# Ordering the work of an attention loop: from one fixed round per step to an order written by a planner with costs and due times

## The chip, the core and the metric

The kernel runs on one core of a Trainium2 chip. The core has five instruction streams that matter here: TensorE (PE in the profile, with PEld for its weight loads), VectorE (DVE), ScalarE (ACT), GpSimd (POOL) and SyncE (SP), which issues the transfers. Each stream executes its own instructions strictly in the order in which the program wrote them, and waits on semaphores for the other streams. The metric is the device time of one execution in microseconds (us), the median of several runs. Lower is better.

## What is computed

One block: a layer norm of `x` (4096 x 512) and of a context (3202 x 512), cross attention with 8 heads of 64, a residual, a second layer norm, and then a small recurrence over the 4096 rows. All of it is in 32-bit floats.

```python
x = _layernorm(builder_state, g1, beta1)
base_n = _layernorm(base_state, g1, beta1)
scores = jnp.einsum('bhqd,bhkd->bhqk', q, k) * (1.0 / np.sqrt(HD))
attn = jax.nn.softmax(scores, axis=-1)
out = jnp.einsum('bhqk,bhkd->bhqd', attn, v)
x = residual + out.reshape(q_in.shape) @ W_o.T + b_o
U = (_layernorm(x, g2, beta2) @ W_in.T + b_in) @ Bmat
s = silu(s @ A.T) + u_t            # 4096 steps in a row, 64 states
x = residual + states @ Cmat + mod
```

The change leaves every one of these operations, with its operands and shapes, as it is.

## The kernel before, in words

**Three parts.** First the keys and values of all 3202 context rows are made and stored in device memory (up to about 260 us of the span). Then comes the attention loop, to about 2510 us. Last, the recurrence runs, with what is left of the last rows (to 2587 us).

**The attention loop.** The 4096 queries are cut into 8 blocks Q of 512; a block has 4 pairs of heads (hp) and 2 halves of 256 queries. One (Q, hp, half) is a *unit*: 64 units. The keys are cut into 13 chunks of 2 x 123 or 2 x 124. One chunk of one unit is a *step*: 832 steps. A step has these pieces, each on one engine:

- `scores` (L465, PE): four matmuls of q and k into a PSUM tile `s` of two banks; there are two such tiles. In the trace a 32-bit matmul is two records, so a piece is x8.
- then a copy of `s` into an SBUF tile `p` (L475, ACT). Up to 20 tiles `p` are alive (NDC + LAG + 4).
- `running` (L486, DVE): the running maximum `top` of the unit, from `s` and the last `top`. It waits for the copy. When it is done, the PSUM tile is free.
- `subtract` (L520, DVE): `p` less the maximum of the unit, `mb`, which lies in PSUM.
- `weights` (L530, ACT): the exponential in place, and, in the same function, `acc` (L539, POOL): the sum of the exponentials over the chunks, an add of 123 x 1024 numbers. The first chunk needs none, so a unit has 12.
- `product` (L548, PE): four matmuls of `p` and v into the PSUM tile `po`. Then `p` is free.

The subtraction needs the maximum over all 13 chunks, so a unit's second half of work (subtract, weights, product) runs 16 to 18 steps (NDC + LAG) behind its scores. Between them lies, once per unit, `maximum`: eight transposes `tt` (L497), two reductions (L504), four transposes `mb` (L512). After a unit's last product comes `finish`: `po` copied (L595, ACT), the two halves of `acc` added (`both`, L598, POOL), transposes `pd` (L604), a reciprocal (L609, L610), a spread (`wide`, L612, ACT), transposes `rb` (L617), a multiplication (L623, DVE).

**Background work.** Per block Q there are two streams. `queries(Q + 1)` loads and normalizes four tiles of x, transposes them (L141) and makes the q of the next block: four times sixteen records `pq` (L180). `project(Q)` takes four tiles of 128 rows through: load, POOL add of `rowb` (L635), matmuls `pa` with the output weights (L638), DVE add (L647), layer norm, POOL add of `modb` (L650), store on SP's queue (L656), transposes `tp_y`, copy (L660), matmuls `pu` (L667), DVE (L671).

**What sets the order.** One Python loop over the steps g, the *round*, writes for each g the same list: the loads of k (4 steps ahead) and v, `running` of step g-1, `weights` of step g-17, `scores` of g, `subtract` of g-16, `product` of g-18, and then at most one portion of each background stream (`background`, which takes the next `yield` of a generator; a stream holds a PSUM tile `m` at most across one portion). So each engine gets its work in the round's fixed order, PE always scores, product, background, and so again; nothing looks at costs.

**Names the change touches.** `queries`, `normalize`, `scores`, `running`, `maximum`, `weights`, `product`, `finish`, `project`, the loop itself. The loop is L1020. The tail (`main_scan` L867, `last_rows` L906) is left, but for how its first pieces are written out.

Of the kernel before, what the change touches and what calls it, by code (L numbers as in the profile page):

```python
# [1 line left out]

# [6 lines left out]
F32 = mybir.dt.float32  # L9
# [21 lines left out]
L = 16  # L31
# [5 lines left out]

def keys(c):
    return CK if c < GC else CK - 1


def key0(c):
    return c * (CK - 1) + min(c, GC)


@with_exitstack
def xattn_ssm_kernel(
# [64 lines left out]
    def normalize(xt, n, name, later=False, pool=None):  # L112
# [5 lines left out]
        nc.vector.bn_aggr(mv[:n], st[:n])  # L118
        ve = pool.tile([P, 1], F32, tag="ve", name=f"ve_{name}")
# [6 lines left out]
        )  # L126

        def scaled():
            xh = pool.tile([P, H], F32, tag="xh", name=f"xh_{name}")
            nc.scalar.activation(  # L130
                xh[:n], xt[:n], AF.Identity, bias=nmr[:n], scale=rstd[:n]
            )
            return xh

        return scaled if later else scaled()
# [16 lines left out]
    def queries(Q, fetched=None):  # L152

        xns = []
        for half in range(2):
            xn = xnp.tile([P, NC, QU], F32, tag="xn", name=f"xn_{Q}_{half}")
            xns.append(xn)
            for t in range(NT // 2):
                r = Q * QB + half * QU + t * P
                if fetched:  # L160
                    xt = fetched[:, half * (NT // 2) + t, :]
                else:
                    xt = xp_.tile([P, H], F32, tag="x", name=f"x_{r}", bufs=3)
                    nc.sync.dma_start(xt, x[r : r + P, :])
                    yield False
                scaled = normalize(xt, P, f"x{r}", later=True)
                yield False
                yield False
                xh = scaled()
                yield False  # L170
                tp = transposes(ps_m, "m", xh, P, f"x{r}")
                yield True
                nc.scalar.copy(xn[:, :, t * P : (t + 1) * P], tp)
                yield False
                yield False
        for hp in range(NC):
            pq = ps_m.tile([P, 512], F32, tag="m", name=f"pq_{Q}_{hp}")
            for half in range(2):
                for i in range(NC):
                    nc.tensor.matmul(  # L180
                        pq[:, half * QU : (half + 1) * QU],
                        wq[:, i, hp * P : (hp + 1) * P],
                        xns[half][:, i, :],
                        start=(i == 0),
                        stop=(i == NC - 1),
                    )
            yield True
            t = qp.tile([P, QB], F32, tag="q", name=f"q_{Q}_{hp}")
            nc.scalar.activation(
                t, pq, AF.Identity, bias=bias[:, hp : hp + 1], scale=HD**-0.5  # L190
            )
            qt[Q, hp] = t
            yield False
# [50 lines left out]
    def side():  # L244
# [95 lines left out]
        yield from queries(0, x0)  # L340
# [117 lines left out]
    def scores(w, c):  # L458
# [3 lines left out]
        for b in range(2):  # L462
            for a in range(2):
                r = slice(a * HD, (a + 1) * HD)
                nc.tensor.matmul(  # L465
                    s[:n, a, b, :],
                    kts[(*w["at"][:2], c)][r, b * n : (b + 1) * n],
                    q[r],
                    start=True,
                    stop=True,  # L470
                )
        t = sp_.tile([CK, 2, 2, QU], F32, tag="s", name=f"p_{w['name']}_{c}")
        w["s"][c] = t
        w["ps"] = s
        nc.scalar.copy(t[:n], s[:n])  # L475

    def running(w, c):

        n, s = keys(2 * c), w["ps"]
        if c == 0:  # L480
            w["top"] = w["s"][0]
            return
        before = w["top"]
# [4 lines left out]
    def maximum(w):  # L488

        m = small.tile([P, 2, 2], F32, tag="m", name=f"m_{w['name']}")  # L490
        tps = []
        for t in range(2):
            tp = ps_m.tile([P, 2, 2, CK], F32, tag="m", name=f"tt_{w['name']}_{t}")
            tps.append(tp)
            for a in range(2):
                for b in range(2):
                    nc.tensor.transpose(  # L497
                        tp[:, a, b, :],
                        w["top"][:, a, b, t * P : (t + 1) * P],
                        ident[:CK, :CK],  # L500
                    )
        yield
        for t in range(2):
            nc.vector.tensor_reduce(  # L504
                m[:, t, :], tps[t].rearrange("p a b k -> p a (b k)"), AX.X, ALU.max
            )
        yield
        mb = ps_b.tile([P, 2, QU], F32, tag="b", name=f"mb_{w['name']}")
        w["mb"] = mb
        for t in range(2):  # L510
            for a in range(2):
                nc.tensor.transpose(  # L512
                    mb[:CK, a, t * P : (t + 1) * P],
                    m[:, t, a : a + 1].to_broadcast([P, CK]),
# [12 lines left out]
    def weights(w, c):  # L527
# [3 lines left out]
        if w["last"] and c in PE_SUMS:  # L531
            return
        before = w.get("acc")
        if before is None:
            w["acc"] = t
            return
# [4 lines left out]
    def product(w, c):  # L541

        n, t = keys(2 * c), w["s"].pop(c)
# [11 lines left out]
        if w["last"] and c in PE_SUMS:  # L555

            if c == PE_SUMS[0]:
                w["pd"] = ps_m.tile([P, 512], F32, tag="m", name=f"pd_{w['name']}")
            sums(w["pd"], t, n, c == PE_SUMS[0], False)
# [29 lines left out]
    def finish(w):  # L589

        Q, hp, half = w["at"]
        name = w["name"]
# [3 lines left out]
        acc = w["acc"]  # L596
        both = accp.tile([CK, 2, QU], F32, tag="both", name=f"both_{name}", bufs=1)
        nc.gpsimd.tensor_tensor(both, acc[:, :, 0, :], acc[:, :, 1, :], ALU.add)  # L598
        yield False
        yield False  # L600
        pd = ps_m.tile([P, 2, 2, CK], F32, tag="m", name=f"pd_{name}")
        for t in range(2):
            for a in range(2):
                nc.tensor.transpose(  # L604
                    pd[:, t, a, :], both[:, a, t * P : (t + 1) * P], ident[:CK, :CK]
                )
        yield True
        rd = small.tile([P, 2, 2], F32, tag="rd", name=f"rd_{name}")
        nc.vector.tensor_reduce(rd, pd, AX.X, ALU.add)  # L609
        nc.vector.reciprocal(rd, rd)  # L610
        wide = op.tile([P, 2, 2, HD], F32, tag="rd", name=f"wide_{name}", bufs=1)
        nc.scalar.copy(wide, rd.unsqueeze(3).to_broadcast([P, 2, 2, HD]))  # L612
        yield False
        yield False
        rb = ps_m.tile([P, 512], F32, tag="m", name=f"rb_{name}")
        for t in range(2):
            nc.tensor.transpose(  # L617
                rb[:, t * P : (t + 1) * P],
                wide[:, t].rearrange("p a d -> p (a d)"),
                ident,  # L620
            )
        yield True
        nc.vector.tensor_tensor(o, o, rb[:, :QU], ALU.mult)  # L623
        yield False

    def project(Q, tiles=range(NT), wait=0):

        for _ in range(wait):
            yield False
        for t in tiles:  # L630
            r = Q * QB + t * P
            xt = xp_.tile([P, H], F32, tag="x", name=f"xr_{r}", bufs=3)
# [552 lines left out]
```

## Time and profile before

| what | value |
|---|---|
| median of 3 runs (lowest to highest) | 2588.69 us (2587.82 to 2590.74) |
| the profiled execution's own time; its span | 2589.05 us; 2587.3 us |
| granted TensorE clock over the span | 0.994 |
| first and last GpSimd `acc` of the loop (start, end) | 300.35 us, 2508.64 us |
| busy from 296 to 2506 us (2210 us): PE, DVE, ACT, POOL | 2153.93, 2033.98, 1738.95, 2013.60 us |
| `acc` adds on POOL in the loop | 698 + 64, 2366 and 2373 ns a record |
| `scores` and `product` on PE | 6656 records each (832 pieces of 8) |

How to read it: the span is the time from the first to the last instruction of one profiled execution; 1.75 us of its own time lie outside the span. "Busy" is the time in which an engine has an instruction in flight. A matmul's end is modelled in the records and matmuls overlap, so how long PE takes for a piece is read from the start of one piece to the start of the next. A bracket behind a row tells how long the engine was idle ahead of it, and which instruction ended the wait.

### The profile page before, as it was taken

How to read it: one execution, taken by the hardware profiler on the slowest of the kernel's cores; microseconds unless marked ns; L12 is line 12 of the kernel's file. 1: busy time of each engine (PE TensorE's matmuls, PEld its weight loads, DVE VectorE, ACT ScalarE, POOL GpSimd, SP SyncE). 2: the span in 40 equal slices, each digit the busy share in tenths (PEclk: the TensorE clock that was granted, in tenths of full speed). 3: DMA queues.
4: the chain of work that ended last, by engine and by line, in shares of the span. 5: the costliest groups of instructions: out<-in, count | busy, mean ns of one | idle time of the engine just before them, and what ended most of it. 6: DMA issues, size and time to landing. Idle time of an engine off the chain costs nothing.

```text
span 2587.3 us, 44495 instructions
## 1 busy us (share of the span) xinstructions
PE 2477.1 (96%) x16648; PEld 1413.6 (55%) x16648; DVE 2137.3 (83%) x2322; ACT 1843.2 (71%) x2111; POOL 2074.9 (80%) x1195
## 2 busy tenths in 40 slices
PE   7989799999999999999999999999999999999987
PEld 3445456555565556555555556555655556555544
DVE  2220797998979997999979897999799997999975
ACT  2232686887868787877878786878787787878753
POOL 1020397999979997999979997999899997999973
PEclk9999999999999999999999999999999999999998
DMA  4422221121211221122212121122112221233364
GB/s 128 137 87 68 84 64 52 54 62 50 84 30 55 65 70 47 56 64 72 64 50 62 51 81 32 54 65 70 48 53 63 76 64 48 77 113 105 110 167 142
DMA packets 178036, 189.23 MB, mean 73 GB/s; under 512 B 14252, under 2 KB 151256, under 8 KB 177818
## 3 DMA queue, kind: packets, MB, share of 16 engines
q1 hardware_dynamic: 173270, 178.67, 23.4%
q10 hardware_dynamic: 4548, 7.67, 1.0%
q8 instruction: 135, 2.21, 0.4%
q14 instruction: 83, 0.68, 0.1%
HBM read 156.40 MB, written 29.89 MB: 72 GB/s over the span
## 4 chain that ended last, share of the span: by engine, by line
PE 50%; DVE 27%; issue 11%; ACT 8%; DMA 2%; POOL 1%; SPq 1%; ACTq 0%; DVEq 0%; POOLq 0%
DVE top L486 17%; PE s L465 15%; PE po L548 13%; DVE p L520 6%; PE pq L180 4%; PE pa L638 4%; ACT p L475 4%; PE pv L394 3%; PE pk L420 2%; ACT p L530 2%; PE tt L497 2%; PE mb L512 1%; DVE rd L609 1%; PE pu L667 1%; POOL acc L539 1%
## 5 line engine op out<-in xcount | busy, mean ns | idle before, releaser
L539 POOL TENSOR_TENSOR acc<-p,acc 123x1024 f32<-123x1024 f32 x698 | 1651.7, 2366 | 100.4 <-ACT p L530 57.8
L475 ACT COPY p<-s 123x1024 f32<-123x1024 f32 (+1 forms) x832 | 834.1, 1003 | 283.9 <-PE s L465 271.1
L520 DVE TENSOR_TENSOR p<-p,mb 123x1024 f32<-123x1024 f32 (+1 forms) x832 | 1001.2, 1210 | 0.8 <-PE mb L512 0.7
L465 PE MATMUL s<-q,k 64*123 64x256 f32 (+1 forms) x6656 | 943.5, 402 | 60.3 <-DVE top L486 48.3
L530 ACT ACTIVATE p<-p 123x1024 f32<-123x1024 f32 (+1 forms) x832 | 879.9, 1058 | 143.2 <-DVE p L520 137.3
L486 DVE TENSOR_TENSOR top<-s,top 123x1024 f32<-123x1024 f32 x704 | 856.7, 1217 | 143.5 <-ACT p L475 135.1
L548 PE MATMUL po<-p,v 123*64 123x256 f32 (+1 forms) x6656 | 900.5, 392 | 0.5 <-ACT o L595 0.5
L465 PEld LDWEIGHTS s<-q,k 64*123 64x123 f32 (+1 forms) x6656 | 561.6, 182 | 373.8 <-DVE top L486 167.6
L548 PEld LDWEIGHTS po<-p,v 123*64 123x64 f32 (+1 forms) x6656 | 404.3, 136 | 399.9 <-issue 222.8
L539 POOL TENSOR_TENSOR acc<-p,p 124x1024 f32<-124x1024 f32 x64 | 151.9, 2373 | 149.4 <-ACT p L530 149.1
L120 POOL TENSOR_SCALAR ve_c<-mv_c 123x1 f32<-123x1 f32 (+1 forms) x26 | 5.8, 225 | 143.9 <-DVE mv_c L118 114.2
L180 PE MATMUL pq<-xn,wq 128*128 128x256 f32 x512 | 117.9, 383 | 0.0
L364 DVE COPY ct<-tp_c 128x492 f32<-128x492 f32 (+1 forms) x13 | 8.7, 672 | 127.4 <-PE tp_c L141 127.4
L638 PE MATMUL pa<-wo,o 128*128 128x512 f32 x240 | 111.0, 605 | 0.0
L486 DVE TENSOR_TENSOR top<-s,p 124x1024 f32<-124x1024 f32 x64 | 77.9, 1217 | 39.4 <-DMA k<-kd 38.1
L180 PEld LDWEIGHTS pq<-xn,wq 128*128 128x128 f32 x512 | 94.8, 190 | 20.5 <-issue 6.3
L394 PE MATMUL pv<-wv,ct 128*123 128x512 f32 (+1 forms) x208 | 97.5, 614 | 0.2 <-ACT vs L403 0.2
L428 ACT ACTIVATE ks<-pk,bias 128x492 f32<-128x492 f32 (+2 forms) x28 | 18.0, 642 | 111.8 <-PE pk L420 59.1
L420 PE MATMUL pk<-ct,wk 128*128 128x492 f32 (+2 forms) x224 | 89.2, 550 | 0.0
L598 POOL TENSOR_TENSOR both<-acc 124x512 f32<-124x512 f32 x63 | 80.7, 1282 | 4.9
L504 DVE TENSOR_REDUCE m<-tt 128x2 f32<-128x496 f32 x128 | 79.9, 665 | 0.7 <-PE tt L497 0.7
L638 PEld LDWEIGHTS pa<-wo,o 128*128 128x128 f32 x240 | 43.1, 189 | 54.6 <-issue 51.5
(182 smaller groups left out, 1361.9 us busy)
## 6 DMA issues: line engine op xcount, KB each, us to landing
k<-kd SPq DMA_DIRECT2D x396, 123.0 KB
v<-vd SPq DMA_DIRECT2D x396, 123.0 KB
k<-kd SPq DMA_DIRECT2D x72, 124.0 KB
v<-vd SPq DMA_DIRECT2D x72, 124.0 KB
xr<-in_x_dram SPq DMA_DIRECT2D x32, 256.0 KB
x1d<-xr SPq DMA_DIRECT2D x32, 256.0 KB
x<-in_x_dram SPq DMA_DIRECT2D x28, 256.0 KB
cx<-in_ctx_dram SPq DMA_DIRECT2D x22, 246.0 KB
```

The lines of the kernel that those rows point to most:

```text
L180: nc.tensor.matmul(pq[:, half * QU : (half + 1) * QU], wq[:, i, hp * P : (hp + 1) * P], xns[half][:, i, :], start=(i == 0), stop=(i == NC ...
L394: nc.tensor.matmul(pv[:n, :H], ct[:, i, o : o + n], wv[:, i, :], start=(i == 0), stop=(i == NC - 1),)
L420: nc.tensor.matmul(pk[:, :n_g], wk[:, i, hp * P : (hp + 1) * P], ct[:, i, :n_g], start=(i == 0), stop=(i == NC - 1),)
L465: nc.tensor.matmul(s[:n, a, b, :], kts[(*w["at"][:2], c)][r, b * n : (b + 1) * n], q[r], start=True, stop=True,)
L475: nc.scalar.copy(t[:n], s[:n])
L486: nc.vector.tensor_tensor(w["top"][:n], s[:n], before[:n], ALU.max)
L520: nc.vector.tensor_tensor(t[:n], t[:n], w["mb"][:n].unsqueeze(2).to_broadcast([n, 2, 2, QU]), ALU.subtract,)
L530: nc.scalar.activation(t[:n], t[:n], AF.Exp)
L539: nc.gpsimd.tensor_tensor(w["acc"][:n], t[:n], before[:n], ALU.add)
L548: nc.tensor.matmul(w["po"][a * HD : (a + 1) * HD, 0, :], vts[(*w["at"][:2], c)][:n, b, a * HD : (a + 1) * HD], t[:n, a, b, :], start=(c == ...
L598: nc.gpsimd.tensor_tensor(both, acc[:, :, 0, :], acc[:, :, 1, :], ALU.add)
L638: nc.tensor.matmul(pa, o_t[Q, c, t // 2][:, t % 2 * P : (t % 2 + 1) * P], wo[:, c, :], start=(c == 0), stop=(c == NC - 1),)
```

## The change

The round is replaced by a list of *pieces*. For every piece the code states its engine, a cost in ns, the pieces it must follow, a due time, and which ring buffers it takes and gives back (`s` 2, `m` 2, `p` 20, and so on: the counts of buffers are those of before). `Plan.order()` then plays the whole loop through, engine by engine, in the program that builds the kernel: whenever an engine is free, it takes, among the pieces whose predecessors are done and whose buffers are free, the one with the earliest due time. The order in which pieces were taken is the order in which the instructions are written. On the chip each engine still runs its list strictly in that order.

On PE a piece after one of another kind is booked with START = 215 ns, after one of the same kind (scores after scores, product after product) with AGAIN = 90 ns; and a ready piece of the same kind as the last is preferred (6000 ns off its due time), up to two in a row. A result is taken to be seen by another engine LATE ns after its end.

Due times are in steps of 2600 ns. The scores of step g are due at g, its subtraction 16 steps later, its product 2.4 steps after that. Background pieces are due at regular distances: one tile of x or of rows each 12 steps, one head pair's q each 6 steps, while the round took their portions as fast as it could. `weights` and the POOL add become two pieces, as do the scores and their copy, and the two halves of the maximum. Loads of k and v hang on the scores and product pieces as before (4 steps ahead; v now 11 ahead of the product, 9 ahead of the subtraction before, which is the same place). Loads of x and stores of rows are pieces of SP.

The diff, cut to its core (generators turned into lists of pieces with the same instructions are left out):

```diff
+STEP = 2600
+QSTEP, RSTEP = 12 * STEP, 12 * STEP
...
+    LATE = {"PE": 110, "DVE": 130, "ACT": 110, "POOL": 100, "SP": 3000}
+    START, AGAIN = 215, 90
...
+        while len(out) < len(pieces):
+            for e in self.LATE:
+                if free[e] > now:
+                    continue
+                best = None
+                for p in ready[e]:
+                    if fits(p):
+                        more = p["kind"] and p["kind"] == last and run < 2
+                        key = p["due"] - (6000 if more and e == "PE" else 0), p["at"]
+                        if best is None or key < best[0]:
+                            best = key, p
+                if best is None:
+                    continue
+                p = best[1]
+                ready[e].remove(p)
+                cost = p["cost"]
+                if e == "PE":
+                    same = p["kind"] and p["kind"] == last
+                    cost += (self.AGAIN if same else self.START) if p["kind"] else 0
+                    last, run = p["kind"], run + 1 if same else 1
...
+            plan.add(("heads", Q, hp), "PE", 1850, head, copied, d, ["m", "q"],
+                     [("xn", ("query", Q, t, "turn")) for t in (0, 2)])
...
+            plan.add((*k, "load"), "SP", 60, load, [from_(d - 4 * STEP)], d - 4 * STEP, ["x"])
+            plan.add((*k, "row"), "POOL", 1280, row, [(*k, "load")], d - STEP)
+            plan.add((*k, "outs"), "PE", 1850, outs, [("scale", i) for i in units_] + [(*k, "row")], d, ["m", "x1"],
+                     [("o_", ("output", i)) for i in units_])
...
+            plan.add((*k, "store"), "SP", 60, store, [(*k, "mod")], d + 3 * STEP, [],
+                     [("x", (*k, "load"))])
...
+        for c in range(NDC):
+            d = (s0 + c) * STEP
+            q = [("q", Q, hp)] if Q else []
+            plan.add(("scores", i, c), "PE", 860, partial(scores_, c), q, d, ["s"],
+                     [("q", ("heads", Q, hp))], "scores")
+            plan.add(("keep", i, c), "ACT", 990, partial(keep, w, c), [("scores", i, c)], d + 1000,
+                     ["p"], [("s", ("scores", i, c))])
+            if c:
+                plan.add(("top", i, c), "DVE", 1145, partial(running, w, c),
+                         [("keep", i, c), ("top" if c > 1 else "keep", i, c - 1)], d + 2000,
+                         ["top"] if c == 1 else [], [("s", ("scores", i, c))])
...
+        for c in range(NDC):
+            d = (s0 + c + NDC + LAG) * STEP
+            plan.add(("less", i, c), "DVE", 1145, partial(subtract, w, c), [("everywhere", i)], d,
+                     [], [("b", ("everywhere", i))])
+            plan.add(("weights", i, c), "ACT", 1050, partial(weights, w, c), [("less", i, c)],
+                     d + 1200)
+            p = ("p", ("keep", i, c))
+            plan.add(("product", i, c), "PE", 860, partial(product_, c),
+                     [("weights", i, c)] + ([("product", i, c - 1)] if c else []),
+                     d + 2 * STEP + 1000, [] if c else ["o"], [p], "product")
...
+                plan.add(("add", i, c), "POOL", 2380, partial(add, w, c),
+                         [("weights", i, c), ("weights" if c == 1 else "add", i, before)], d + 2400,
...
-        for g in range(len(steps) + NDC + LAG + 2):
-            b = g - NDC - LAG
...
-            if 3 in ends and sub:
-                subtract(*sub)
-            if prev:
-                running(*prev)
-            if exp:
-                weights(*exp)
...
-            if now:
-                scores(*now)
-            if 3 not in ends and sub:
-                subtract(*sub)
...
-            if mul:
-                product(*mul)
...
-            background(more=1 not in ends)
...
+        for piece in plan.order():
+            piece()
```

## The prediction, as it went on record

> **What bounds the kernel now.** I read the busy shares first, then one whole block of 8 units cut at its `both` adds (stage by stage), then the rows of PE, POOL and DVE inside those stages, and last the waits.
>
> ```profile
> PE 2477.1 (96%) x16648; PEld 1413.6 (55%) x16648; DVE 2137.3 (83%) x2322; ACT 1843.2 (71%) x2111; POOL 2074.9 (80%) x1195
> ```
>
> PE looks full. But eight units in a row are not alike (columns: stage, its length, then busy us of PE, PEld, DVE, ACT, POOL):
>
> ```profile
> 1162.68:1198.12 35.44, 35.44 (x256) 20.84 (x258) 32.99 (x36) 28.04 (x33) 33.11 (x18) 1.00 0.23 71
> 1198.12:1234.56 36.44, 36.44 (x264) 20.71 (x262) 34.44 (x39) 28.89 (x34) 34.12 (x21) 1.00 0.22 63
> 1234.56:1267.84 33.28, 31.81 (x244) 18.11 (x241) 32.71 (x36) 28.74 (x34) 31.67 (x19) 1.00 0.24 72
> 1267.84:1301.36 33.52, 31.85 (x220) 20.22 (x221) 27.94 (x29) 24.24 (x28) 30.61 (x16) 1.00 0.19 52
> 1301.36:1344.01 42.65, 41.76 (x296) 25.55 (x296) 33.55 (x33) 31.38 (x36) 29.67 (x14) 1.00 0.13 38
> 1344.01:1374.93 30.92, 29.82 (x228) 16.88 (x228) 30.69 (x31) 26.14 (x29) 29.66 (x14) 1.00 0.21 56
> 1374.93:1405.85 30.92, 29.82 (x228) 16.89 (x228) 30.69 (x31) 26.14 (x29) 29.64 (x14) 1.00 0.21 60
> 1405.85:1443.49 37.64, 37.64 (x254) 20.62 (x252) 33.71 (x37) 26.92 (x30) 36.48 (x23) 1.00 0.22 65
> ```
>
> Units with background work take 35 to 43 us and PE has no gap in three of them; two units without any take 30.92 us. What holds those two is in POOL's rows:
>
> ```profile
> 1344.01 1.28 POOL L598 TENSOR_TENSOR both<-acc 124x512 f32<-124x512 f32 x1
> 1345.24 2.38 POOL L539 TENSOR_TENSOR acc<-p,p 124x1024 f32<-124x1024 f32 x1
> 1347.70 4.82 POOL L539 TENSOR_TENSOR acc<-p,acc 123x1024 f32<-123x1024 f32 x2
> 1352.91 21.94 POOL L539 TENSOR_TENSOR acc<-p,acc 123x1024 f32<-123x1024 f32 x9 [0.40 <-ACT p L530]
> ```
>
> Nine adds in 21.94 us: (21.94 - 2.37) / 8 = 2.446 us from start to start, 0.08 more than the record. 12 x 2.446 + 1.23 = 30.6 of 30.92 us. So light units are bound by POOL and heavy ones by PE, and the fixed round can't trade one for the other. DVE shows how stiff it is, in the unit with the two dense `pq` groups:
>
> ```profile
> 1303.40 1.23 DVE L486 TENSOR_TENSOR top<-s,top 123x1024 f32<-123x1024 f32 x1 [3.76 <-ACT p L475]
> 1304.54 1.21 DVE L520 TENSOR_TENSOR p<-p,mb 124x1024 f32<-124x1024 f32 x1
> 1309.13 1.23 DVE L486 TENSOR_TENSOR top<-s,top 123x1024 f32<-123x1024 f32 x1 [3.38 <-ACT p L475]
> ```
>
> DVE sits 3.4 us behind a `top` whose scores are queued behind 3.65 us of `pq`, while it has subtractions to come.
>
> **The change, part by part.**
>
> *Same work.* No instruction of compute is added or removed, so every gain is idle time or PE's cost of switching.
>
> *Pairs on PE.* The switching cost is in three places of PE's rows: alternating, two scores side by side early in the loop, and two products in the tail.
>
> ```profile
> 1341.23 1.13 PE L465 MATMUL s<-q,k 64*123 64x256 f32 x8
> 1342.29 1.08 PE L548 MATMUL po<-p,v 123*64 123x256 f32 x8
> 1343.30 1.13 PE L465 MATMUL s<-q,k 64*123 64x256 f32 x8
> ```
>
> ```profile
> 290.96 1.99 PE L465 MATMUL s<-q,k 64*124 64x256 f32 x16
> ```
>
> ```profile
> 2488.97 1.95 PE L548 MATMUL po<-p,v 123*64 123x256 f32 x16
> ```
>
> Scores then product: 1.06 us to the next start; product then scores: 1.01. Two scores: 1.99 - 1.13 = 0.86. Two products: 1.95 - 1.08 = 0.87. A pair of each saves 0.20 + 0.14 = 0.34 us per two steps; 416 x 0.34 = 141 us if every step were paired. Will they pair? A second score needs both `s` tiles free. A tile is held from its matmuls through copy and `top`: about 0.86 + 0.1 + 1.0 + 1.2, so the second tile of a pair is free some 4.3 us after the first score of that pair at best, when DVE has no other piece in between. Two steps at today's mean take 2208 / 416 = 5.3 us. One DVE piece (1.14) in the wrong place and the tile is late; the product is then taken alone. Products pair more easily (due 2.4 steps after their subtraction). Bounds: none, or all. I take half, 71 us.
>
> *Evening out.* Background is due each 6 or 12 steps in place of as fast as the round allows. The load of each engine over the loop, 300.35 to 2508.64 us (2208 us, first to last `acc`):
> POOL: 762 adds x 2.446 = 1864; 63 `both` x 1.23 = 78; 62 adds of 128x512 (L635, L650, L778) x 1.23 = 76; 58 norms x (0.30 + 0.66 + 0.22) = 68; in all 2087, so 121 idle. PE: busy 2154 of 2210 between 296 and 2506, 56 idle. DVE 2034, 176 idle. The most that this change can give is POOL's 121 us: 2468 us. PE reaches it only if its own 2154 shrink, so evening out alone is worth no more than PE's 56, and pairs are what opens the rest.
> Sum: PE's work 2154 - 71 = 2083, plus idle as today, 56 (new order, but new misfits too), makes 2139 for 2210: -71. POOL then idles 50 of 2137 us; its best stage today (30.6 of 30.92) idles 1%, so 2.4% over mixed stages is believable.
>
> Here a rule of the Trainium skill would mislead. Perfetto Trace Analysis, Identifying the Most-Contended Engine, holds occupancy to be a fair measure of how close VectorE and GpSimd are to their limit. POOL's occupancy, 2013.6 of 2210, would leave 196 us; counted from start to start, 121 are left. I use the row; by the rule the floor would be 2393 us. For PE the same section calls matmul busy time a poor measure because matmuls are pipelined; that side the rows bear out: 97% busy, and yet 0.2 us can be had from each pair.
>
> *Wrong prices.* The plan books a head pair's q and a row tile's `pa` at 1.85 us. The rows say 3.65 and 3.63 (117.9 / 32 = 3.68 and 111.0 / 30 = 3.70 by busy time):
>
> ```profile
> L180 PE MATMUL pq<-xn,wq 128*128 128x256 f32 x512 | 117.9, 383 | 0.0
> L638 PE MATMUL pa<-wo,o 128*128 128x512 f32 x240 | 111.0, 605 | 0.0
> ```
>
> 28 + 30 pieces x 1.8 = 104 us of PE that the plan doesn't know of, and 762 x 0.066 = 50 us of POOL (booked 2.38). Against it stand scores and products booked long: alternating 2 x 1.075 for 2.07, paired 2 x 0.95 for 1.73, or 67 to 90 us over 832 steps. Net, PE is under-booked by 14 to 37 us, but in lumps: behind each of the 58 pieces ACT's copy and DVE's `top`, next in their lists, come 1.8 us late, and what is queued behind them too. POOL covers that: with 20 tiles `p`, 13 of them the unit's own and about 3 in flight, some 4 adds (9.8 us) can lie ready. Cover there: 0; cover gone: 104. I take 0 on top of the 56 kept as idle.
>
> *SP.* The store of rows waits for POOL's add of `modb`, and loads of k and v queue behind it. Today that wait is already up to 20 us long (231.9 us in 18 waits between 500 and 2300 us) and no score waits for a k there, since k is asked for 4 steps (10.6 us) ahead. The new place is right behind the add in planned time. I take 0; if POOL lags by more than that cover, about 2 us x 15 row tiles (half the units load k) = 30. Moving x loads and splitting `weights` from `add` cost nothing: the same instructions on queues with idle time (ACT 1739 of 2210). The tail after 2508 us, 80 us, is left as it is; its first pieces may shift by a few us either way.
>
> **The rivals.**
> 1. *Pairs seldom form.* DVE frees the `s` tiles one at a time, each 2.3 us, and PE takes what is ready, alternating. Then PE's 2154 stay and only idle shrinks, by half: -28, 2561 us. For it: the tight 4.3 of 5.3 us above. Against: products wait with late due times, so after a late score both kinds lie ready.
> 2. *At POOL's floor.* With two thirds of the pairs or more PE's work is 2154 - 94 = 2060, under POOL's 2087. With 1% idle, as in POOL's best stage, the loop takes 2108: -100, 2489 us.
> 3. *Slower: the frozen order is wrong where prices are.* Priced by its own costs the plan has POOL at 762 x 2.38 + 63 x 1.28 + 60 x 1.28 + 58 x 1.05 = 2032; with 50 idle, 2082. If all 104 + 50 us of missing price land on the path, since three engines near their limits run in one strict order, the loop takes 2236 for 2208: 2617 us. It is slower than before from 126 of the 154 us on. For it: PE, DVE and POOL all over 90% busy, so a delay meets little slack. Against: POOL's stock of 4 adds, and the matmuls booked long.
> 4. *The order comes out much as before*, the same PE chain: 2584 to 2594.
>
> **How the numbers follow.** 2589.05 - 71 = 2518 us; the median of the runs, 2588.69, stands 0.4 under the profiled time, which changes nothing at this scale. Chances: this forecast (2490 to 2545) 0.50; rival 1 (2545 to 2583) 0.18; rival 2 0.08; rival 4 0.05; rival 3 0.19. About 0.2% (5 us) is what a measurement of this kernel can tell from no change. So faster 0.76, same 0.05, slower 0.19. The range 2490 to 2605 leaves out rival 2 and rival 3 where most of the missing price counts.
>
> **What would show it.** Right: rows of scores and products x16 in PE's timeline of the middle of the loop, about half of all; PE's busy time near 2083; no unit of 42 us and none under 30.6; DVE's 3.4 us waits at `pq` gone or under 2. Wrong: PE idle well over 56 us with waits of scores on `top` (pairs planned but blocked), POOL waiting on ACT over 60 us, scores waiting on k loads (SP), or x8 rows throughout.

## The result, and the profile after

The changed kernel takes 2546.36 us (median of 4 runs, 2544.55 to 2549.87) beside 2588.26 us for the kernel before on the same chip: a ratio of 0.9838 [0.9821, 0.9855], 42 us less. The forecast was 71 us less. The direction, the engine that sets the end and the mechanism were as forecast; the gain was 0.6 of it, and the time lies 1.4 us above the 2490 to 2545 us that the forecast gave to its own case. The profiled run took 2546.95 us (2545.1 us span, clock 0.995), which is 42.1 under the profiled run of before.

Busy shares first, from the top of the page of after:

```profile
PE 2439.3 (96%) x16648; PEld 1435.7 (56%) x16648; DVE 2128.5 (84%) x2322; ACT 1838.7 (72%) x2111; POOL 2071.1 (81%) x1195
```

Still 96%: the share cannot show the gain, since PE's work and the span shrank together. The loop itself, from the first to the last `acc`, does. Its row for before, then for after (stretch, length, busy us of PE, PEld, DVE, ACT, POOL with instruction counts, clock, DMA share, GB/s):

```profile
300.35:2508.64 2208.29, 2153.47 (x15476) 1248.22 (x15478) 2029.63 (x2077) 1735.44 (x1914) 2016.16 (x1061) 1.00 0.23 66
```

```profile
299.34:2464.38 2165.04, 2118.69 (x15490) 1272.18 (x15488) 2020.33 (x2077) 1731.36 (x1915) 2012.37 (x1061) 1.00 0.23 67
```

The loop lost 43.2 us: PE's busy time 34.8, and PE's idle time (length less busy) 8.4, from 54.8 to 46.4. The head is 1.0 us shorter, the tail 2.1 longer. Now PE's timeline inside one unit of after (start, us, engine, line, tiles, records):

```profile
1321.99 1.99 PE L576 MATMUL s<-q,k 64*123 64x256 f32 x16
1323.91 1.95 PE L660 MATMUL po<-p,v 124*64 124x256 f32 x16
1325.80 1.13 PE L576 MATMUL s<-q,k 64*123 64x256 f32 x8
1326.86 1.08 PE L660 MATMUL po<-p,v 123*64 123x256 f32 x8
```

A pair of scores (x16) takes 1.92 us to the next start, and two single ones 2 x 1.06; a pair of products 1.89 where two single ones take 2 x 1.01. Right behind them the order alternates again. Counted over the loop, neighbours of one kind rose from 16 to 163 for scores and from 8 to 131 for products, of 416 possible each. These are the numbers that the plan has.

The same block of 8 units as before, cut at its `both` adds (same columns as the loop's rows):

```profile
1142.91:1180.56 37.65, 36.17 (x266) 21.33 (x262) 34.99 (x39) 29.63 (x34) 36.31 (x24) 1.00 0.22 68
1180.56:1220.14 39.58, 39.41 (x274) 23.36 (x274) 36.94 (x42) 30.80 (x36) 36.27 (x23) 1.00 0.19 58
1220.14:1251.73 31.59, 31.18 (x242) 18.55 (x240) 30.93 (x34) 27.74 (x32) 30.50 (x21) 1.00 0.34 102
1251.73:1283.27 31.54, 30.82 (x232) 18.41 (x231) 31.01 (x33) 26.62 (x30) 30.56 (x17) 1.00 0.15 42
1283.27:1311.58 28.31, 28.31 (x183) 19.95 (x182) 19.59 (x20) 19.50 (x22) 27.22 (x14) 1.00 0.09 26
1311.58:1350.69 39.11, 38.66 (x302) 23.12 (x301) 37.11 (x37) 30.72 (x33) 29.68 (x14) 1.00 0.21 59
1350.69:1382.31 31.62, 29.95 (x231) 17.36 (x231) 31.48 (x32) 26.94 (x30) 29.64 (x14) 1.00 0.19 60
1382.31:1417.44 35.13, 34.76 (x256) 20.70 (x254) 33.64 (x36) 28.00 (x33) 34.23 (x20) 1.00 0.21 64
```

The eight take 274.5 us for 280.8, but they are hardly more alike: 28.3 to 39.6 us now, 30.9 to 42.7 before. The lump of `pq` is still there: in the stretch of 28.31 us PE is busy without a gap while DVE does only 19.59 us of work. DVE's row behind the last `pq` is no better than the one of before:

```profile
1309.89 1.23 DVE L597 TENSOR_TENSOR top<-s,top 123x1024 f32<-123x1024 f32 x1 [4.11 <-ACT p L589]
```

It waits 4.11 us for a copy whose scores are queued behind `pq`, where 3.76 and 3.38 were seen before.

### The profile page after: what moved, and what is told of

The parts are those of the page before. It is cut to its first block, busy times and chain, and to the rows that moved or that the text cites. A ratio compares the mean times of both kernels' runs of the same rounds, so it can differ in the third digit from the quotient of the medians.

```text
span 2545.1 us, 44356 instructions
## 1 busy us (share of the span) xinstructions
PE 2439.3 (96%) x16648; PEld 1435.7 (56%) x16648; DVE 2128.5 (84%) x2322; ACT 1838.7 (72%) x2111; POOL 2071.1 (81%) x1195
## 4 chain that ended last, share of the span: by engine, by line
PE 52%; DVE 23%; issue 9%; ACT 6%; POOL 5%; DMA 3%; SPq 1%; ACTq 0%; POOLq 0%; DVEq 0%
PE s L576 16%; DVE top L597 14%; PE po L660 13%; DVE p L633 6%; POOL acc L651 5%; PE pq L270 4%; PE pa L848 4%; ACT p L589 3%; PE pv L505 3%; PE pk L531 3%; PE tt L605 2%; ACT p L643 2%; DMA x<-in_x_dram 2%; PE mb L625 1%; PE pu L894 1%
## 5 line engine op out<-in xcount | busy, mean ns | idle before, releaser
L651 POOL TENSOR_TENSOR acc<-p,acc 123x1024 f32<-123x1024 f32 x698 | 1651.1, 2366 | 65.3 <-ACT p L643 24.4
L576 PE MATMUL s<-q,k 64*123 64x256 f32 (+1 forms) x6656 | 907.5, 398 | 43.9 <-DVE top L597 31.9
L597 DVE TENSOR_TENSOR top<-s,top 123x1024 f32<-123x1024 f32 x704 | 856.1, 1216 | 53.1 <-ACT p L589 50.8
L660 PE MATMUL po<-p,v 123*64 123x256 f32 (+1 forms) x6656 | 880.1, 391 | 3.8 <-ACT p L643 2.7
L576 PEld LDWEIGHTS s<-q,k 64*123 64x123 f32 (+1 forms) x6656 | 574.3, 182 | 336.9 <-DVE top L597 152.1
L660 PEld LDWEIGHTS po<-p,v 123*64 123x64 f32 (+1 forms) x6656 | 416.7, 136 | 364.8 <-issue 154.8
L651 POOL TENSOR_TENSOR acc<-p,p 124x1024 f32<-124x1024 f32 x64 | 152.2, 2378 | 128.6 <-DMA k<-kd 77.6
L716 POOL TENSOR_TENSOR both<-acc 124x512 f32<-124x512 f32 x63 | 80.8, 1283 | 2.4
L605 PE MATMUL tt<-ident,top 124*128 124x124 f32 x512 | 73.8, 278 | 9.0 <-DVE top L597 7.2
```

Source lines behind the costliest of these rows:

```text
L576: nc.tensor.matmul(s[:n, a, b, :], kts[(*w["at"][:2], c)][r, b * n : (b + 1) * n], q[r], start=True, stop=True,)
L597: nc.vector.tensor_tensor(w["top"][:n], s[:n], before[:n], ALU.max)
L605: nc.tensor.transpose(tp[:, a, b, :], w["top"][:, a, b, t * P : (t + 1) * P], ident[:CK, :CK],)
L651: nc.gpsimd.tensor_tensor(w["acc"][:n], t[:n], before[:n], ALU.add)
L660: nc.tensor.matmul(w["po"][a * HD : (a + 1) * HD, 0, :], vts[(*w["at"][:2], c)][:n, b, a * HD : (a + 1) * HD], t[:n, a, b, :], start=(c == ...
```

## The experiments

All figures of the loop in one table; each ratio is against the kernel before, run on the same chip (its median there lies between 2588.26 and 2590.58 us). The loop goes from the first to the last `acc` of the profiled execution. "Pairs" are neighbours of one kind on PE, scores / products.

| kernel | median us | ratio, interval | loop | PE busy | PE idle | pairs |
|---|---|---|---|---|---|---|
| before | 2588.26 | 1 | 2208.3 | 2153.5 | 54.8 | 16 / 8 |
| after | 2546.36 | 0.9838 [0.9821, 0.9855] | 2165.0 | 2118.7 | 46.4 | 163 / 131 |
| no_pairs | 2584.53 | 0.9981 [0.9972, 0.9991] | 2202.5 | 2149.8 | 52.7 | 28 / 76 |
| neutral | 2560.41 | 0.9888 [0.9871, 0.9904] | 2178.3 | 2141.4 | 36.9 | 55 / 76 |
| spread_round | 2576.54 | 0.9954 [0.9938, 0.9971] | 2195.0 | 2150.0 | 45.0 | 16 / 8 |
| pairs_round | 2771.73 | 1.0706 [1.0688, 1.0724] | 2388.6 | 2107.8 | 280.8 | 361 / 418 |
| dense | 2564.67 | 0.9904 [0.9887, 0.9920] | 2181.3 | 2123.2 | 58.0 | 157 / 89 |
| held | 2548.04 | 0.9835 [0.9819, 0.9852] | 2164.0 | 2117.9 | 46.1 | 165 / 138 |
| prices | 2550.06 | 0.9852 [0.9835, 0.9868] | 2167.5 | 2116.4 | 51.1 | 181 / 146 |
| pe_light | 2480.63 | 0.9584 [0.9568, 0.9600] | 2100.5 | 2026.6 | 73.9 | 163 / 131 |
| pool_light | 2544.84 | 0.9824 [0.9808, 0.9841] | 2156.4 | 2110.7 | 45.6 | 163 / 131 |
| sbuf_top | 3153.08 | 1.2178 [1.2158, 1.2199] | 2772.9 | 2273.8 | 499.0 | 258 / 73 |
| sbuf_top_round | 3216.41 | 1.2417 [1.2396, 1.2437] | 2840.3 | 2349.5 | 490.8 | 16 / 8 |
| sbuf_top_prices | 3154.08 | 1.2178 [1.2158, 1.2199] | 2776.7 | 2278.7 | 498.0 | 231 / 105 |

My theory: the gain is PE's switching cost, saved where the planner finds pairs, and a smaller part is evener background work. The rivals: evening out alone does it; or the planner's wrong prices eat most of what pairs bring.

**Pairs put off instead of sought (no_pairs).** The planner of after, with the preference turned round:

```diff
+def same_(p):
+    return p["kind"] and p["kind"] == last
...
-more = p["kind"] and p["kind"] == last and run < 2
-key = p["due"] - (6000 if more and e == "PE" else 0), p["at"]
+key = p["due"] + (6000 if same_(p) and e == "PE" else 0), p["at"]
```

> The planner as it is, but a piece of the same kind as the last on PE is put off by 6000 ns in place of preferred: the planned order then has 28 + 76 neighbouring pairs of scores and of products where the change has 163 + 131. If pairs pay (0.20 and 0.14 us each), 135 x 0.20 + 55 x 0.14 = 35 us come back: about 2581 us, PE busy 35 us higher. If the free choice of order and the even spread of the background work pay, it stays at 2546 within 8 us.

Its loop:

```profile
302.39:2504.88 2202.49, 2149.84 (x15480) 1256.27 (x15480) 2024.38 (x2077) 1736.70 (x1915) 2014.14 (x1061) 1.00 0.23 66
```

37 of the 42 us are gone (4.7 are left against the kernel before on the same chip), and PE's busy time is back at 2149.8. The pairs left are those in which nothing else was ready, or nothing else was due within 6 us of them. This doesn't show that pairs are 37 us of the gain: pushing a due piece back also spoils the order (PE idle 52.7 for 46.4). The next run separates that.

**Pairs neither sought nor put off (neutral).** The 6000 are taken away, and both prices of the switch are 215.

```diff
-    START, AGAIN = 215, 90
+    START, AGAIN = 215, 215
...
-key = p["due"] - (6000 if more and e == "PE" else 0), p["at"]
+key = p["due"] - 0, p["at"]
```

> The planner with no opinion on pairs: no preference for the same kind, and START and AGAIN both 215. Planned pairs 55 + 76 (the change 163 + 131; with pairs put off 28 + 76). If pairs pay: 108 x 0.20 + 55 x 0.14 = 29 us above the change, 2575 us. If putting pairs off had only spoilt the order, and the change's gain came from its free order: within 8 us of 2546.

```profile
298.44:2476.73 2178.29, 2141.44 (x15480) 1258.50 (x15482) 2023.67 (x2078) 1733.55 (x1915) 2013.40 (x1061) 1.00 0.23 67
```

Neither case came: 2560.4 lies between the 2554 of the one and the 2575 of the other. Order by due time alone gives 28 of the 42 us: PE idle 36.9, 18 less than before, and PE busy 12.1 less, with 39 + 68 more pairs, which come about by themselves. The preference then adds 14: PE's busy time falls by another 22.7 (108 + 55 more pairs) and 9.5 of idle come back; the likely reason, not tested by itself, is that a pair is taken ahead of what is due. So two thirds of the gain come without any search for pairs, though part of that is pairs too.

**Evening out without a planner (spread_round).** The kernel before, where a queries stream now lets seven rounds pass, instead of one, after each head pair's q (from the second block on):

```diff
-            yield False
+            for _ in range(7 if Q else 1):
+                yield False
```

> The kernel before, with 7 rounds instead of 1 between two of the four dense q groups of a block, so that they lie some 20 us apart in place of 6. No pairs, no planner. If evening out is what pays: half of the change's gain or more, 2565 us or less. If pairs pay, evening out reaches only PE's idle time: 2575 to 2588 us.

13 us faster than the kernel before on the same chip (7 to 16 by the interval), with not one pair more: PE's idle time falls from 54.8 to 45.0, its busy time by 3.5. So in the fixed round evening out is real, and is the smaller part: 29 of the 42 us are not had by it.

**Pairs without a planner (pairs_round).** The kernel before, with products and background of an even g held until after the scores of the odd one.

```diff
-            if mul:
+            todo.append(mul)
+            if g % 2 == 0:
+                mine = []
+            else:
+                mine, todo = todo, []
+            for mul in mine:
+                if not mul:
+                    continue
...
-            background(more=1 not in ends)
+            late.append(1 not in ends)
+            if g % 2:
+                for more_ in late:
+                    background(more=more_)
+                late = []
```

> The kernel before, with its fixed round, but two steps at a time: the product and the background portions of an even step are written after the scores of the odd step, so PE runs scores, scores, product, product, background. No planner. If pairs pay by themselves: up to 350 pairs of each kind, PE's work falls by up to 119 us, and POOL's 2087 us with 2 to 3% idle sets the end: 2520 to 2550 us. If the fixed order of DVE and ACT keeps the second scores of a pair waiting for its PSUM tile: 2590 us or more, with waits of scores on top.

183 us slower than before, with 361 and 418 pairs. PE's timeline:

```profile
1405.05 1.13 PE L465 MATMUL s<-q,k 64*123 64x256 f32 x8
1406.82 1.13 PE L465 MATMUL s<-q,k 64*123 64x256 f32 x8 [0.63 <-PE s L465]
1407.88 1.95 PE L548 MATMUL po<-p,v 123*64 123x256 f32 x16
1409.75 1.13 PE L465 MATMUL s<-q,k 64*123 64x256 f32 x8
1411.29 1.13 PE L465 MATMUL s<-q,k 64*124 64x256 f32 x8 [0.41 <-DVE top L486]
```

and its waits (who waits for whom: us in all, times, longest):

```profile
POOL acc L539 <- ACT p L530: 368.4, 200, 78.0
...
DVE top L486 <- ACT p L475: 256.3, 203, 7.1
...
PE s L465 <- DVE top L486: 108.5, 126, 2.7
```

The second score of a pair waits for its PSUM tile, which `top` has not given back, and everything behind it on PE waits too. Of 344 score pairs with complete records only 170 run back to back. A pair with a wait inside shows as two x8 rows and advances PE by 2.19 us (1.13 to the end of the first row and 1.06 to the next start), more than two single scores (2.12). These waits are not all of it: of PE's 281 us of idle time in the loop 98 are waits of scores for `top`, 61 stand ahead of scores with no releaser in the trace, and in 41 a product waits for the copy of `po`. This is the forecast's "pairs planned but blocked"; the planner avoids most of it, because in its own clock it takes a second score only when the tile is free: in after 13 of 148 score pairs in the loop have a wait inside.

**Background crowded (dense).** After, with background due three times as densely:

```diff
-QSTEP, RSTEP = 12 * STEP, 12 * STEP
+QSTEP, RSTEP = 4 * STEP, 4 * STEP
```

> The planner as it is, but background pieces are due each 4 (rows, x) or 2 (q) steps in place of each 12 or 6. The planned pairs are 157 + 89 (163 + 131). If pairs pay: 42 fewer product pairs x 0.14 = 6 us more, about 2552. If the even spread pays: 2565 us or more.

17 us of the 42 are lost, 16 of them in the loop: 11.6 in PE idle, 4.5 in PE busy (42 fewer product pairs). That is the second case to within 0.4 us, so the place of the background in the order is a part of the change. Which background pieces cost it is open.

**The lump of `pq` spread (held).** A head pair's q may start at most two steps ahead of its due time, and a step is 2540 ns.

```diff
-STEP = 2600
+STEP = 2540
...
+            if p["name"][0] == "heads" and now < p["due"] - 2 * STEP:
+                return False
```

> The planner, but a q group may not be taken earlier than 2 steps ahead of its due time, and a step is 2540 ns; in the change all four are taken 35 to 65 us early, 5 to 6 us apart, as soon as PE has nothing else, and they leave DVE 12 of 28 us idle in that unit. Planned pairs 165 + 138 as in the change; the four groups 13 to 17 us apart. If lumps cost: up to DVE's and POOL's idle there, some 4 us per block, 7 blocks: 2520 us. If not: 2546 within 8 us.

The groups of `pq` in one block, from PE's timeline of this run:

```profile
1289.69 3.72 PE L272 MATMUL pq<-xn,wq 128*128 128x256 f32 x16
...
1307.79 3.62 PE L272 MATMUL pq<-xn,wq 128*128 128x256 f32 x16
...
1321.81 3.62 PE L272 MATMUL pq<-xn,wq 128*128 128x256 f32 x16
...
1337.30 3.72 PE L272 MATMUL pq<-xn,wq 128*128 128x256 f32 x16
```

14 to 18 us apart, where after has them at 1281.19, 1288.55, 1295.35 and 1302.95. The time is that of after (the intervals lie on each other). So the lump, and DVE's 4.1 us wait in it, cost nothing that this run can show: PE works without a gap there. Two things changed at once, though, the hold and the step; a gain of one could hide a loss of the other.

**The prices set right (prices).**

```diff
-    START, AGAIN = 215, 90
+    START, AGAIN = 175, 0
...
-            plan.add(("heads", Q, hp), "PE", 1850, head, copied, d, ["m", "q"],
+            plan.add(("heads", Q, hp), "PE", 3650, head, copied, d, ["m", "q"],
...
-            plan.add((*k, "outs"), "PE", 1850, outs, [("scale", i) for i in units_] + [(*k, "row")], d, ["m", "x1"],
+            plan.add((*k, "outs"), "PE", 3630, outs, [("scale", i) for i in units_] + [(*k, "row")], d, ["m", "x1"],
...
-                plan.add(("add", i, c), "POOL", 2380, partial(add, w, c),
+                plan.add(("add", i, c), "POOL", 2446, partial(add, w, c),
```

> The planner with the prices of the trace: q groups 3650, pa groups 3630, acc adds 2446, START 175, AGAIN 0. Planned pairs 181 + 146. If the missing 29 us of the forecast went to the wrong prices: 2520 us or less. If the order that comes out is no better for true prices: 2540 to 2560 us.

No gain: 2550.06 us, 18 + 15 more pairs, and 4.7 more of PE idle. In this planner the wrong prices ate nothing that right ones give back.

**Less work on PE (pe_light).** The `pq` groups after the first block and the `pa` groups use two of their four slices of the contraction.

```diff
-            for i in range(NC):
+            for i in range(NC if Q == 0 else 2):
...
-                for c in range(NC):
+                for c in range(2):
```

> The change with its order untouched, but q of blocks 1 to 7 and the output projection are summed over two of four slices only (the output is not the reference's): each of these 58 groups then takes about the 1.85 us that it was booked at, and PE has 104 us less work. If PE with its switching sets the end: the loop falls by 50 us or more, to 2495 us or less, where POOL's 2087 us stop it near 2475. If POOL or DVE set it: 2530 us or more.

```profile
298.31:2398.81 2100.50, 2026.57 (x15150) 1205.45 (x15148) 2015.49 (x2077) 1729.35 (x1915) 2014.03 (x1061) 1.00 0.24 69
```

PE's busy time falls by 92.1 and the loop by 64.5, so PE was what set the end. It stops at 2100.5 us, 13.5 above the 2087 that the forecast worked out for POOL from start to start. POOL's busy time there is 2014.03, which by itself would leave 86 us free. The trace divides these 86: 59.8 are gaps under 0.15 us between one POOL record and the next, and only 26.7 are waits, all for ACT:

```profile
POOL acc L651 <- ACT p L643: 26.7, 33, 1.6
```

So POOL's own work takes 2074 us of the loop, and it is idle for 1.3% of it, less than PE (73.9 us) or DVE (79.7).

**Less work on POOL (pool_light).** The adds of the chunks after the first take only half of their columns.

```diff
-nc.gpsimd.tensor_tensor(w["acc"][:n], t[:n], before[:n], ALU.add)
+h = slice(0, 2) if c == 1 else slice(0, 1)
+nc.gpsimd.tensor_tensor(w["acc"][:n, :, h], t[:n, :, h], before[:n, :, h], ALU.add)
```

> The change with its order untouched, but of each unit's 12 adds on POOL, 11 (last unit fewer) add half of the columns only (the output is not the reference's): POOL has about 840 us less work. If PE sets the end, as forecast, with POOL waiting on it: 2530 to 2546 us. If POOL holds the loop in its light units, as in the kernel before: 2510 us or less.

```profile
299.65:2456.03 2156.38, 2110.74 (x15446) 1267.89 (x15444) 2020.02 (x2076) 1731.73 (x1914) 1254.48 (x1061) 1.00 0.23 67
```

```profile
POOL acc L652 <- ACT p L643: 757.1, 442, 79.2
```

Against after, POOL works 758 us less in the loop, and the ratios of the two kernels lie within each other's interval. (The loop's row is 8.7 us shorter because it ends with a POOL add, which is now short; PE's last product ends only 2.4 us sooner.) In the loop POOL waits 677.9 us for ACT, which is the 757.1 less one wait of 79.2 ahead of its first add; after has 75.3 there. In after, POOL is close to the bound but isn't it.

**The `s` tile given back earlier (sbuf_top, and the same in the round and with the prices).** `running` reads the SBUF copy in place of the PSUM tile, so that the tile is free when the copy is done.

```diff
-nc.vector.tensor_tensor(w["top"][:n], s[:n], before[:n], ALU.max)
+nc.vector.tensor_tensor(w["top"][:n], w["s"][c][:n], before[:n], ALU.max)
...
-                         ["top"] if c == 1 else [], [("s", ("scores", i, c))])
+                         ["top"] if c == 1 else [], [])
```

> The planner, but the running maximum reads the SBUF copy of the scores in place of the PSUM tile, which is then free after ScalarE's copy, one DVE piece earlier. Planned pairs of scores 258 (163), of products 73 (131). If the s tiles limit the pairs, and pairs pay: 95 x 0.20 - 58 x 0.14 = 11 us of switching less and fewer waits of scores on top (17 us between 500 and 2260 us): 2515 to 2537 us. If VectorE with both inputs in SBUF and GpSimd's reads shut each other out: adds well over 2.45 us from start to start, 2600 us or far more.

> The same edit in the kernel before, with its fixed round: no pairs can come of it. If only pairs pay: 2580 to 2590 us. If a shorter chain from scores to the next free tile pays by itself, the waits of scores on top go (48 us in all): 2550 to 2570 us. If the SBUF reads clash: as above.

> The running maximum from SBUF together with the prices of the trace. Planned pairs 231 + 105. If the SBUF reads don't clash: 2505 to 2530 us, the best version. If they do: as slow as the edit without prices.

The first line alone, in the kernel before, is sbuf_top_round; both lines with the costs of prices are sbuf_top_prices. All three are over 560 us slower than before. Two groups of after first (busy us, mean ns of one; then idle before, with what ended it):

```profile
L651 POOL TENSOR_TENSOR acc<-p,acc 123x1024 f32<-123x1024 f32 x698 | 1651.1, 2366 | 65.3 <-ACT p L643 24.4
L597 DVE TENSOR_TENSOR top<-s,top 123x1024 f32<-123x1024 f32 x704 | 856.1, 1216 | 53.1 <-ACT p L589 50.8
```

The groups of sbuf_top, POOL's:

```profile
L651 POOL TENSOR_TENSOR acc<-p,acc 123x1024 f32<-123x1024 f32 x698 | 2091.2, 2997 | 79.9 <-ACT p L643 40.2
...
L716 POOL TENSOR_TENSOR both<-acc 124x512 f32<-124x512 f32 x63 | 136.0, 2159 | 0.9
```

and DVE's:

```profile
L597 DVE TENSOR_TENSOR top<-p,top 123x1024 f32<-123x1024 f32 x704 | 1415.4, 2011 | 28.0 <-ACT p L589 24.5
L633 DVE TENSOR_TENSOR p<-p,mb 123x1024 f32<-123x1024 f32 (+1 forms) x832 | 992.8, 1207 | 11.9 <-PE mb L625 11.4
```

The score pairs did rise, from 163 to 258, so the hold of `top` on the `s` tile is what limits them. But `top` with both inputs in SBUF takes 2011 ns for 1216, and POOL's add 2997 for 2366, while the subtraction, whose second input `mb` lies in PSUM, keeps its 1207. The fixed round pays much the same, so it is the form of the operation and not the order. Is it two SBUF inputs by themselves, or POOL at work beside them? POOL's first add starts at 295.22 us, and until then sbuf_top's DVE groups are:

```profile
L597 DVE TENSOR_TENSOR top<-p,top 123x1024 f32<-123x1024 f32 x14 | 17.1, 1223 | 1.6 <-ACT p L589 0.4
L597 DVE TENSOR_TENSOR top<-p,p 124x1024 f32<-124x1024 f32 x2 | 2.4, 1220 | 37.4 <-DMA k<-kd 37.4
```

The same instruction costs 1.22 us while POOL is idle, and 2.24 in the median where POOL works for 90% of it or more. The other way round, the 42 adds of POOL with no `top` beside them take 2.36 us in the median and the others 3.2. So the two engines hold each other up. PE's granted clock, 0.92 to 0.94 in these runs, is no cause of it: DVE and POOL slow down only side by side, and PE is idle for over 490 us. The Trainium skill has the mechanism: SBUF — State Buffer, Who interferes with whom, says that a VectorE instruction with two SBUF inputs contends with a GpSimd instruction that reads SBUF. The rows agree.

## Why the forecast was right, and where it was off

**PE is the bound, POOL the floor 2087: right.** pe_light and pool_light show both sides. Counting POOL from start to start was the right count, 13 us too high: the trace of pe_light gives 2074, and the loop stopped at 2100.5, while POOL's busy time would have allowed 2014. DVE was not tested in this way. It holds 23% of the chain that ended last in after (27% before), and its `top` gives the `s` tiles back.

**The price of a pair: right.** In after, pairs that run back to back advance PE by 1.92 us (scores) and 1.88 us (products) in the median, single pieces by 1.06 and 1.015: 0.20 and 0.15 saved, as forecast (0.20 and 0.14).

**The number of pairs: this is the term that failed.** "I take half, 71 us" meant 208 of each kind. The planner made 163 and 131, of which 16 and 8 were there before: 147 x 0.20 + 123 x 0.14 = 46.6 us. How far scores and products move the end of PE's work fell by 24.3 + 12.3 = 36.6. Of the remaining 10, some 6 went to pairs with a wait inside, which save nothing: 13 of 148 score pairs (10 wait for `top`) and 8 of 85 product pairs (all wait for ACT's exponential). So the mean score pair advances PE by 1.956 us, not 1.92. The rest is mostly single pieces that advance PE a little more than before (scores 1.081 us for 1.074 in the mean). Other pieces together cost PE some 2 us more; among them are the transposes `tt` (73.8 us of records for 68.2), whose two halves the planner now takes apart. So PE's work fell by 34.8, not 71. The condition that the forecast named was the limiting one ("one DVE piece in the wrong place and the tile is late"); half was too hopeful a share of it. The groups show the same from the other side, first in the kernel before, then in the one after:

```profile
L465 PE MATMUL s<-q,k 64*123 64x256 f32 (+1 forms) x6656 | 943.5, 402 | 60.3 <-DVE top L486 48.3
L548 PE MATMUL po<-p,v 123*64 123x256 f32 (+1 forms) x6656 | 900.5, 392 | 0.5 <-ACT o L595 0.5
```

```profile
L576 PE MATMUL s<-q,k 64*123 64x256 f32 (+1 forms) x6656 | 907.5, 398 | 43.9 <-DVE top L597 31.9
L660 PE MATMUL po<-p,v 123*64 123x256 f32 (+1 forms) x6656 | 880.1, 391 | 3.8 <-ACT p L643 2.7
...
L605 PE MATMUL tt<-ident,top 124*128 124x124 f32 x512 | 73.8, 278 | 9.0 <-DVE top L597 7.2
```

These rows are of the whole span. Of PE's 46.4 us of idle time in the loop 30.8 still lie ahead of scores, and in 22.6 of them the trace names `top` as what ended the wait (39.6 of 54.8 before).

**PE idle kept at 56: nearly right, and for the reason given.** It fell by 8.4. neutral shows that it would have fallen by 18 with no preference for pairs: order by due time closes gaps, and with the preference some are open again.

**These errors add up to the miss:** PE's work 36 us short, its idle 8 better than forecast, head and tail 1 worse: 29. The total is as near as it is partly by luck: the gain in idle time, which the forecast did not count on, covers a part of the pairs that did not come.

**Evening out of the units: the mechanism is real, the signs named for it came only in part.** spread_round and dense show that the place of the background in the order matters, by 13 and 17 us. "No unit of 42 us" came true: the longest in the whole loop is 39.9 us, where the kernel before has seven of 42.6. "None under 30.6" did not: six units take 28.3 to 29.3 us. Nor did "DVE's 3.4 us waits gone or under 2", though they became rare: `top` waits more than 2 us for its copy 5 times, 4.1 us each, where it did so 28 times before, 3.4 to 3.8 us each. I had read a due time as a date; in this planner it is only a priority. Whatever is ready goes as soon as PE is free, so the four `pq` groups still come within 26 us. The floor of 30.6 counts 12 adds and holds only where a stretch has 12: the stretch of 28.31 us has 11, since the first add of its unit ran ahead of the cut. The four `pq` groups close together cost the fixed round 13 us (spread_round), and held finds no cost of them in the planner's order.

**Wrong prices at 0, against rival 3's 154: right.** With the prices mended the time is the same. One sum is not exact: "67 to 90" for scores and products booked long has 85 for half of the pairs and 104 for all, by the same prices; the 0 does not rest on it. That the stock of `p` tiles covers a late piece, as the forecast said, agrees with the waits: in after POOL waits for ACT less than before (206.9 us there, of which 78.9 in one wait; after has one of 77.6 as well, put down to the first load of k), and only a little over the line of 60:

```profile
POOL acc L651 <- ACT p L643: 75.3, 44, 7.6
```

**SP at 0: right.** Its longest wait for the `modb` add is 15.4 us (between 500 and 2200 us), and the only scores that wait for a k are the first two of the loop, 3.8 us in all, as in the kernel before (3.9).

```profile
SPq L865 <- POOL xr L862: 175.8, 19, 15.4
```

**The rivals.** Rival 1, pairs seldom with idle halved, gave 2561, and its stretch of chances (2545 to 2583) is where the measured 2546.36 just falls. Its mechanism is not what happened: PE's work did not stay, it fell by 34.8 us. neutral comes close to that case (fewer pairs, less idle) and took 2560.4, but with 12.1 us of it from PE's work. Rival 2 would have needed two thirds of the pairs.

**Open.** No run that computes the whole result beat the changed kernel beyond noise. More score pairs need the `s` tile sooner without a VectorE operation on two SBUF inputs, or a third tile; neither was tried. No run lightened DVE alone, so how much of the end hangs on `top` is not shown. What made up the rest of pairs_round's loss is open too.

## What to carry to other kernels

When an engine is full and its price depends on what it did just before, count how often the cheaper neighbourhood can form, by the resource that the second piece needs (here the PSUM tile that `top` holds), and not by how many pieces there are. Grouping on one engine pays only if the engines that free its buffers are ordered for it too: looking for pairs gave 14 us of the planner's 42, and forcing them cost 183 in a fixed round. A due time used as a priority holds nothing back, so look for what work is taken early, and then ask whether that costs anything before mending it.

## What the runs showed of the hardware

- Two VectorE inputs in SBUF against GpSimd: `top` 1216 to 2011 ns, `acc` 2366 to 2997, `both` 1283 to 2159; the kernel 22% slower. With GpSimd idle the same `top` takes 1223. One operand in PSUM kept both engines clear of each other in the kernel before, where an add takes 2.36 us without a `top` beside it and 2.37 with one; I hadn't seen that as a reason for its form.
- A wait inside a pair on PE takes its whole gain: a broken pair of scores advances PE by 2.19 us, a whole one by 1.92, two single ones by 2.12.
- In pe_light GpSimd waits for only 26.7 of the loop's 2100.5 us and yet shows 2014.0 busy: 59.8 us lie in gaps under 0.15 us between records, about 0.08 per add.
